# Two products for a column and its mirror image in the forward transforms along y

## The chip, the cores and the metric

The kernel runs on one core of a Trainium2 chip. A core has a matrix engine (TensorE, PE in the profile, with PEld for its weight loads), a vector engine (VectorE, DVE), a scalar engine (ScalarE, ACT), GpSimd (POOL), a queue engine that here issues the transfers (SyncE, SP), and 16 DMA engines. Matrix products land in PSUM, which here is eight banks of 512 fp32 values in each of 128 partitions; everything else is kept in SBUF or, between stages, in HBM. The engines run on their own and wait for each other on semaphores. The metric is the time of one execution on the device in microseconds (us).

## What is computed

The input is 4 images of 128 channels of 128 x 128 pixels. Layer 0 is a state-space layer over windows of 8 x 8 pixels. Layer 1 normalizes over channels and filters in the Fourier domain:

```python
z = (x - mu) / jnp.sqrt(var + 1e-05)
z = z * ln_gamma[None, :, None, None] + ln_beta[None, :, None, None]
Xf = jnp.fft.rfft2(z, axes=(-2, -1))
Phi = Phi_f_real + 1j * Phi_f_imag
Uf = Xf[:, :, None, :, :] * jnp.conj(Phi)[None, None]
U = jnp.fft.irfft2(Uf, s=(gx, gy), axes=(-2, -1))
S = jnp.einsum('bdlxy,lhd->bhxy', U, Theta)
H = jnp.einsum('bdxy,hd->bhxy', S, W1) + b1[None, :, None, None]
H = jax.nn.gelu(H, approximate=False)
out = jnp.einsum('bhxy,dh->bdxy', H, W2) + b2[None, :, None, None]
return x + out
```

What matters here is `rfft2`: for each image and channel a real 128 x 128 picture becomes 128 x 65 complex numbers. A Fourier transform along one axis is a product with a constant matrix of cosines and sines.

## The kernel before

There are four stages, one after the other. `mamba_layer` computes layer 0 and the normalized z, and leaves z in HBM as `zb`. `spectra` makes the forward transforms and leaves them in HBM as `xf`. `mix` multiplies by Theta and Phi for each of the 65 frequencies in y, leaving `sf`. `images_and_mlp` transforms back and applies the two last products. Each stage reads what the one ahead of it has stored. Instructions of an engine run in the order of the program text (`manual_schedule`); the waits between engines are put in by the framework, which tracks tiles. A pool's `bufs` is how many buffers a name rotates through: the next user of a buffer waits for the last reader of its previous content.

`spectra` is the only stage with edited instructions. For each of the four images b it has two parts.

Along x: `load` (line 491, on SP) brings blocks of 16 channels, 128 x 16 x 128 values, 1 MB, from `zb` into one of three z buffers. `along_x` (lines 497 and 498) takes four channels at a time: four matmuls of 128 x 128 into one PSUM bank `p1`, in four rotating banks, and one copy of 128 x 512 into the tile `a`, by ScalarE and VectorE in turn (`copies`, an endless cycle of the two). Channels lie closest in `a`, so the copy writes with a step of 512 bytes. Since z is real, the transform along x is kept as real parts of columns 0 to 64 and imaginary parts of columns 1 to 63: 128 columns of `a`. There are 32 such groups per image. `a` has a single buffer.

Along y: `along_y` (lines 500 to 513) takes three of the 128 output columns k at a time (KG = 512 // 130). For column k it uses m = min(k, 128 - k), the column's number or that of its mirror image, and makes two matmuls that accumulate in PSUM: the real column of `a` against `fy[:, KY : 3 * KY]`, and the imaginary column against one part or another of `fy`, whose sign depends on whether k is m or its mirror image. Columns 0 and 64 have no imaginary part and need one matmul. So an image has 2 + 2 x 126 = 254 matmuls along y, each with 130 result columns: 65 real parts and 65 imaginary parts. The two halves of a group are copied from PSUM to the tile x (line 511), the real parts by ScalarE and the imaginary parts by VectorE, again with a step of 512 bytes at the destination.

The tile x holds 64 columns, so an image has two of them (q = 0 and 1), each stored to `xf` by one DMA of 4160 KB (line 527). SP issues in program order: the loads of an image's first part, then its two stores, each of which waits for its tile x, and then the loads of the next image. Two blocks of the next image are asked for ahead of time, a third as the next image begins.

Of the other stages it is enough that `mix` starts with loads from `xf` (line 555), and that `idft_x`, `Phi_r` and `Phi_i`, constants prepared on the host, are indexed by the column along x.

Of the kernel before, what the change touches and what calls it, by code (L numbers as in the profile page):

```python
# [13 lines left out]
F32 = mybir.dt.float32  # L14
BF16 = mybir.dt.bfloat16
AF = mybir.ActivationFunctionType
ALU = mybir.AluOpType
PSUM = bass.MemoryType.PSUM

P = 128  # L20
# [6 lines left out]
W = 128  # L27
HB = 512
NL = 16
KY = W // 2 + 1  # L30
NG = WS * W // P


def mamba_layer(tc, d, x, x1, zb, deltas, dus):
# [429 lines left out]
def spectra(tc, d, zb, xf):  # L464

    nc = tc.nc  # L470
    B = len(zb)
    DG = 16
    CG, KG = HB // W, HB // (2 * KY)
    WH = W // 2
    with ExitStack() as ctx:
        ctx.enter_context(tc.manual_schedule())
        cp = ctx.enter_context(tc.tile_pool(name="f_const", bufs=1))
        sb = ctx.enter_context(tc.tile_pool(name="f_sb", bufs=2))
        ps = ctx.enter_context(tc.tile_pool(name="f_ps", bufs=4, space=PSUM))
        fx = cp.tile([P, W], F32, tag="fx", name="fx")  # L480
        nc.sync.dma_start(fx, d["dft_x"])
        fy = cp.tile([P, 4 * KY], F32, tag="fy", name="fy")
        nc.sync.dma_start(fy, d["dft_y"])
        loaded = {}
        copies = itertools.cycle((nc.scalar.copy, nc.vector.tensor_copy))

        def load(b, i):
            b, i = b + i // P, i % P
            if b < B:
                loaded[b, i] = sb.tile([P, DG, W], F32, tag="z", name="z", bufs=3)  # L490
                nc.sync.dma_start(loaded[b, i], zb[b][i : i + DG].rearrange("c x y -> x c y"))

        def along_x(b, i, a):
            z = loaded[b, i - i % DG]
            p1 = ps.tile([P, CG, W], F32, tag="p1", name="p_fx")
            for k in range(CG):
                nc.tensor.matmul(p1[:, k], z[:, i % DG + k], fx, start=True, stop=True)
            next(copies)(a[:, :, i : i + CG].rearrange("p k c -> p c k"), p1)

        def along_y(a, x, cols):  # L500
            p2 = ps.tile([P, KG, 2 * KY], F32, tag="p2", name="p_fy")
            for o, k in zip(range(KG), cols):
                m = min(k, W - k)
                single = m % WH == 0
                nc.tensor.matmul(p2[:, o], a[:, m], fy[:, KY : 3 * KY], start=True, stop=single)
                if not single:
                    by = fy[:, : 2 * KY] if m == k else fy[:, 2 * KY :]
                    nc.tensor.matmul(p2[:, o], a[:, WH + m], by, start=False, stop=True)
            n, at = len(cols), cols[0] % WH
            for r in range(2):  # L510
                next(copies)(
                    x[:, :, r, at : at + n].rearrange("p y k -> p k y"), p2[:, :n, r * KY : (r + 1) * KY]
                )

        load(0, 0)
        load(0, DG)
        for b in range(B):
            a = sb.tile([P, W, P], F32, tag="a", name="a", bufs=1)
            for i in range(0, P, CG):
                if i % DG == 0:  # L520
                    load(b, i + 2 * DG)
                along_x(b, i, a)
            for q in range(2):
                x = sb.tile([P, KY, 2, WH], F32, tag="x", name="x")
                for k in range(q * WH, (q + 1) * WH, KG):
                    along_y(a, x, range(k, min(k + KG, (q + 1) * WH)))
                nc.sync.dma_start(xf[:, :, b, q].rearrange("y c r x -> c y r x"), x)


def mix(tc, d, xf, sf):  # L530
# [179 lines left out]
@with_exitstack  # L710
def conv_kernel(ctx: ExitStack, tc: tile.TileContext, d, out):
    x = d["x"]
    B = x.shape[0]

    def images(name):
        return [tc.dram_tile([P, W, W], F32, name=f"{name}_{b}") for b in range(B)]

    x1, zb = images("x1"), images("z")
    xf = tc.dram_tile([KY, P, B, 2, 2, W // 2], F32, name="xf")
    sf = [tc.dram_tile([W, 2, KY, 2, P // 2], F32, name=f"sf_{b}") for b in range(B)]  # L720
    deltas, dus = (
        [[tc.dram_tile([P, WS * W], F32, name=f"{name}_{i}_{ch}") for ch in range(2)] for i in range(2)]
        for name in ("delta", "du")
    )
    mamba_layer(tc, d, x, x1, zb, deltas, dus)
    spectra(tc, d, zb, xf)
    mix(tc, d, xf, sf)
    images_and_mlp(tc, d, sf, x1, out)


def dft():

    w = np.exp(2j * np.pi * (np.outer(np.arange(W), np.arange(W)) % W) / W)
    h = w[:, :KY]

    s = w[:KY] * np.where(np.arange(KY) % (W // 2) == 0, 1, 2)[:, None] / W**2
    parts = {
        "dft_x": (h.real, -h.imag[:, 1:-1]),
        "dft_y": (h.imag, h.real, -h.imag, -h.real),
        "idft_x": (w.real, w.imag),  # L740
    }
    d = {k: np.concatenate(v, 1).astype(np.float32) for k, v in parts.items()}
    rows = np.r_[1 : KY - 1, 0, KY - 1]
    d["idft_y"] = np.concatenate((s.real[rows], -s.imag[rows[:-2]])).astype(np.float32)
    return d


def selectors():

    e = np.tile(np.eye(8), (1, NS))  # L750
    rsel, ssel = np.zeros((4, 4, 8, 4, P)), np.zeros((P, 4, 4, 8))
    for i in range(4):
        rsel[:, i, :, i] = e
        ssel[:, i, i] = e.T
    d = {"rsel": rsel.reshape(P, 4, P), "ssel": ssel.reshape(P, 4, 32), "center": np.eye(P) - 1 / P}
    return {k: v.astype(np.float32) for k, v in d.items()}


def layout(i):

    def col(a):
        return a.reshape(-1, P).T if a.ndim == 1 else a.reshape(-1, P, a.shape[1]).transpose(1, 0, 2)

    d = {"x": i["x"]}
    for k in "ln_g ln_b b_in conv_w conv_b W_x dt_b A_log D W_out b_out".split():
        d[k] = col(i[f"L0_conv_{k}"])
    d["W_in"], d["dt_w"] = i["L0_conv_W_in"], i["L0_conv_dt_w"]
    d["W_in_t"] = col(d["W_in"][:, : 2 * P].T).reshape(P, 2 * P)

    w = d.pop("W_x")  # L770
    d["W_xdt"] = w[..., :DR].transpose(2, 1, 0).reshape(DR, 2 * P)
    d["W_bc"] = np.repeat(w[..., DR:].reshape(P, 2, 2, NS), 8, -1)

    d["A_log"] = i["L0_conv_A_log"].reshape(32, 8, NS).transpose(2, 1, 0).reshape(P, 32)
    d["gamma"], d["beta"] = col(i["L1_conv_ln_gamma"]), col(i["L1_conv_ln_beta"])
    d["Theta"] = i["L1_conv_Theta"].transpose(2, 0, 1)
    d["Phi_r"], d["Phi_i"] = (i[f"L1_conv_Phi_f_{k}"].transpose(1, 0, 2) for k in ("real", "imag"))
    d["W1"], d["W2"] = i["L1_conv_W1"].T, col(i["L1_conv_W2"].T)
    d["b1"], d["b2"] = col(i["L1_conv_b1"]), col(i["L1_conv_b2"])
    return d | dft() | selectors()  # L780
# [18 lines left out]
```

## Time and profile before

| | us |
|---|---|
| median of three runs | 10449.41 |
| lowest and highest | 10445.54, 10451.61 |
| the profiled execution | 10450.79 |
| its span, first to last instruction | 10448.8 |
| window of the layer 0 stage, 0 to 7195 | 7195 |
| window of the forward transforms with the first loads of the next stage, 7195 to 7624 | 429 |
| window of `mix`, 7624 to 9632 | 2008 |
| window of `images_and_mlp`, 9632 to 10449 | 817 |

The span is the time on the engines; the small rest of the profiled execution lies around it. In the window from 7195 to 7624 TensorE is busy for 352.24 us, VectorE for 151.54, ScalarE for 151.89 and GpSimd for 0.00, with DMA at 0.58 of its capacity.

In the profile's lines an instruction is named by the line of the program that issues it, its engine, what it writes and reads, and its count. An entry "idle before" gives how long the engine stood idle just ahead of those instructions, and after the arrow what it was that released it. A matmul in fp32 leaves two records, since the number of records along y is 2032 for four times 254 matmuls. The chain of waits follows the work that ended last backwards: at each step to whatever released it, or to the instruction ahead of it on its engine.

### The profile page before, as it was taken

The numbers are of one execution on the slowest core, as the hardware profiler recorded it, in microseconds if no ns is written. First come the engines' busy times: TensorE is split into PE (matmuls) and PEld (weight loads), VectorE is DVE, ScalarE is ACT, GpSimd is POOL, SyncE is SP. The second block draws the span as 40 slices with busy tenths as digits, with TensorE's granted clock in tenths as the row PEclk, the third lists the DMA queues.
The fourth block names the chain that finished last, engine by engine and source line by source line (L and its number), as shares of the span: only waits on it lengthen the run. The fifth ranks groups of instructions, "written<-read, shape, count | busy, mean of one in ns | idle before, by whom it ended". The sixth has DMA issues, their size and how long they took to land.

```text
span 10448.8 us, 143616 instructions
## 1 busy us (share of the span) xinstructions
PE 9293.9 (89%) x48900; PEld 5027.3 (48%) x48900; DVE 8980.1 (86%) x7234; ACT 6524.3 (62%) x12463; POOL 8231.4 (79%) x4188
## 2 busy tenths in 40 slices
PE   6888888888888888888888888887889999998999
PEld 2333333333333333333333333335889999998766
DVE  5999999999999999999999999995389999998433
ACT  5776777777777777777777677773344444444433
POOL 5899998998998998989989899893079999997000
PEclk8999989989999999999999999997999999999999
DMA  4777677777776776777767767775521111112332
GB/s 150 213 229 220 213 223 218 217 219 219 225 221 213 226 222 214 223 217 225 221 210 228 218 215 223 219 221 160 148 68 34 35 35 36 36 36 62 136 128 93
DMA packets 1168110, 1794.06 MB, mean 172 GB/s; under 512 B 368641, under 2 KB 436497, under 8 KB 1166225
## 3 DMA queue, kind: packets, MB, share of 16 engines
q1 hardware_dynamic: 1167376, 1784.88, 56.6%
q8 instruction: 387, 6.34, 0.3%
q14 instruction: 347, 2.83, 0.1%
HBM read 1481.44 MB, written 303.04 MB: 171 GB/s over the span
## 4 chain that ended last, share of the span: by engine, by line
PE 58%; ACT 20%; DVE 9%; DMA 7%; issue 4%; POOL 1%; SPq 1%; DVEq 0%; ACTq 0%; POOLq 0%
PE p_v L578 13%; DVE hs L410 6%; PE p_du L376 6%; PE p_conv L202 5%; DMA dr<-delta 5%; ACT part L589 5%; PE p_bc L217 5%; PE p_dt L227 4%; PE p_y L428 4%; DVE p_du L408 3%; PE p_out L274 2%; ACT dA L391 2%; PE ln_cen L150 2%; ACT p_du L391 2%; PE p_h L672 2%
## 5 line engine op out<-in xcount | busy, mean ns | idle before, releaser
L418 POOL TENSOR_TENSOR hs<-hs,bc 128x1024 f32<-128x1024 f32 x2048 | 4806.3, 2372 | 408.9 <-DVE hs L410 357.3
L410 DVE TENSOR_TENSOR_SCAN hs<-dA,p_du 128x1024 f32<-128x1024 f32 x1600 | 3659.0, 2287 | 208.2 <-DVE p_du L408 4.9
L591 POOL TENSOR_TENSOR acc<-acc,part 128x512 f32<-128x512 f32 x1430 | 1829.3, 1319 | 640.6 <-ACT part L589 640.6
L408 DVE TENSOR_TENSOR p_du<-p_du,bc 128x1024 f32<-128x1024 f32 x1600 | 1935.8, 1210 | 219.6 <-PE p_du L376 215.0
L391 ACT ACTIVATE dA<-dr,A 128x504 f32<-128x504 f32 x3200 | 2072.0, 704 | 33.1 <-DVE hs L410 23.7
L578 PE MATMUL p_v<-theta,xk 128*128 128x128 f32 x16640 | 1941.4, 277 | 87.9 <-ACT part L589 51.9
L578 PEld LDWEIGHTS p_v<-theta,xk 128*128 128x128 f32 x16640 | 1883.1, 192 | 146.2 <-ACT part L589 118.9
L595 DVE SCALAR_TENSOR_TENSOR acc<-p_v,phi,acc 128x512 f32<-128x512 f32 x2470 | 1672.4, 740 | 114.2 <-PE p_v L578 87.5
L376 PE MATMUL p_du<-du,c_rsel 32*128 32x512 f32 x6400 | 1364.3, 678 | 370.2 <-DVE hs L410 370.2
L589 ACT ACTIVATE part<-p_v,phi 128x512 f32<-128x512 f32 x1430 | 904.8, 686 | 803.9 <-PE p_v L578 800.3
L428 PE MATMUL p_y<-hs,c_ssel 128*32 128x512 f32 x8192 | 1225.7, 634 | 134.2 <-DVE yz L263 82.9
L410 DVE TENSOR_TENSOR_SCAN hs<-p_du,ur 128x1024 f32<-128x1024 f32 x448 | 1019.0, 2275 | 86.8 <-ACT p_du L391 60.5
L356 POOL TENSOR_TENSOR ur<-ur,bc 128x1024 f32<-128x1024 f32 x448 | 1063.1, 2373 | 10.7 <-DMA ur<-du 10.7
L202 PE MATMUL p_conv<-tn,W_conv 128*128 128x512 f32 x2048 | 1007.3, 616 | 3.2 <-ACT xc L207 1.6
L376 PEld LDWEIGHTS p_du<-du,c_rsel 32*128 32x128 f32 x6400 | 370.4, 192 | 1081.1 <-issue 780.6
L227 PE MATMUL p_dt<-xc,W_dt 128*128 128x512 f32 x1024 | 619.8, 736 | 48.0 <-ACT dl L238 42.3
L391 ACT ACTIVATE p_du<-dr,A 128x504 f32<-128x504 f32 x896 | 613.9, 685 | 29.1
L428 PEld LDWEIGHTS p_y<-hs,c_ssel 128*32 128x32 f32 x8192 | 184.3, 111 | 887.5 <-issue 571.2
L207 ACT ACTIVATE xc<-p_conv,b_conv 128x512 f32<-128x512 f32 x256 | 176.2, 688 | 639.3 <-PE p_conv L202 639.3
L245 POOL TENSOR_TENSOR dl<-dl,ab 128x1024 f32<-128x1024 f32 x128 | 302.6, 2364 | 338.5 <-ACT ab L242 338.5
L202 PEld LDWEIGHTS p_conv<-tn,W_conv 128*128 128x128 f32 x2048 | 346.8, 189 | 455.2 <-issue 247.9
L168 PE MATMUL ln_back<-ident,cs 128*128 128x128 f32 x2048 | 339.5, 316 | 222.3 <-ACT cs L162 216.6
(100 smaller groups left out, 10341.0 us busy)
## 6 DMA issues: line engine op xcount, KB each, us to landing
dr<-delta SPq DMA_DIRECT2D x4096, 256.0 KB, 5.2
ur<-du SPq DMA_DIRECT2D x896, 256.0 KB, 6.4
delta<-dl SPq DMA_DIRECT2D x128, 512.0 KB, 2.9
du<-du SPq DMA_DIRECT2D x128, 512.0 KB, 5.4
xf<-x SPq DMA_DIRECT2D x8, 4160.0 KB, 16.4
xk<-xf SPq DMA_DIRECT2D x130, 256.0 KB, 3.8
sf<-acc SPq DMA_DIRECT2D x520, 64.0 KB, 1.7
s<-sf SPq DMA_DIRECT2D x8, 4160.0 KB, 13.4
```

What stands on the lines that cost most here:

```text
L202: nc.tensor.matmul(windows(o.pc), W_conv[:, ch, k], moved, start=(k == 0), stop=(k == K - 1))
L356: nc.gpsimd.tensor_tensor(fetched[s], fetched[s], both(o.bc[0], h), ALU.mult)
L376: nc.tensor.matmul(u.bank[:, j % 2], c["rsel"][p, u.i], half(u.o.du[p, u.ch], u.h), start=True, stop=True)
L391: nc.scalar.activation(u.dA[:, q, :, 1:], u.delta[:, q].rearrange("p (w t) -> p w t", t=L)[:, :, 1:], AF.Exp, scale=A[:, g : g + 1],)
L408: nc.vector.tensor_tensor(u.bu, u.bu, both(u.o.bc[0], u.h), ALU.mult)
L410: nc.vector.tensor_tensor_scan(u.hs.rearrange("p q t -> p (q t)"), u.dA.rearrange("p q w t -> p (q w t)"), u.bu.rearrange("p q t -> p (q t)"),
L418: nc.gpsimd.tensor_tensor(u.hs, u.hs, both(u.o.bc[1], u.h), ALU.mult)
L428: nc.tensor.matmul(o.py[h, ch][32 * j : 32 * j + 32], c["ssel"][:, u.i], units[s + j // 2].hs[:, j % 2], start=(u.i == 0), stop=False, ski ...
L578: nc.tensor.matmul(t[:, b], o.xk[:, b, r], theta[:, k], start=True, stop=True)
L589: nc.scalar.activation(part, v[of], AF.Copy, scale=factor)
L591: nc.gpsimd.tensor_tensor(apart, apart, part, ALU.add)
L595: nc.vector.scalar_tensor_tensor(mine, v[of], factor, mine, ALU.mult, ALU.add)
```

## The change

Column k and its mirror image 128 - k come from the same two products: one is their sum, the other their difference. After the change the two products of a column m from 1 to 63 are made once, each into a bank of its own (`pr` and `pi`), ScalarE copies `pr` to SBUF, VectorE adds `real` and `pi` into the tile x for column m, ScalarE copies `pi` to SBUF, and GpSimd subtracts `imag` from `real` into x for the mirror image. Columns 0 and 64 are made by `lone`.

```diff
-        ps = ctx.enter_context(tc.tile_pool(name="f_ps", bufs=4, space=PSUM))
+        ps = ctx.enter_context(tc.tile_pool(name="f_ps", bufs=3, space=PSUM))
...
-                loaded[b, i] = sb.tile([P, DG, W], F32, tag="z", name="z", bufs=3)
+                loaded[b, i] = sb.tile([P, DG, W], F32, tag="z", name="z", bufs=6)
...
-            p1 = ps.tile([P, CG, W], F32, tag="p1", name="p_fx")
+            p1 = ps.tile([P, CG, W], F32, tag="p1", name="p_fx", bufs=2)
...
         def along_y(a, x, cols):
-            p2 = ps.tile([P, KG, 2 * KY], F32, tag="p2", name="p_fy")
-            for o, k in zip(range(KG), cols):
-                m = min(k, W - k)
-                single = m % WH == 0
-                nc.tensor.matmul(p2[:, o], a[:, m], fy[:, KY : 3 * KY], start=True, stop=single)
-                if not single:
-                    by = fy[:, : 2 * KY] if m == k else fy[:, 2 * KY :]
-                    nc.tensor.matmul(p2[:, o], a[:, WH + m], by, start=False, stop=True)
-            n, at = len(cols), cols[0] % WH
-            for r in range(2):
-                next(copies)(
-                    x[:, :, r, at : at + n].rearrange("p y k -> p k y"), p2[:, :n, r * KY : (r + 1) * KY]
-                )
-
-        load(0, 0)
-        load(0, DG)
+            pr = ps.tile([P, KG, 2 * KY], F32, tag="pr", name="p_fy_r")
+            pi = ps.tile([P, KG, 2 * KY], F32, tag="pi", name="p_fy_i")
+            for o, m in enumerate(cols):
+                nc.tensor.matmul(pr[:, o], a[:, m], fy[:, KY:], start=True, stop=True)
+                nc.tensor.matmul(pi[:, o], a[:, WH + m], fy[:, : 2 * KY], start=True, stop=True)
+
+            def parts(t):
+                return t[:, : len(cols)].rearrange("p k (r y) -> p k r y", r=2)
+
+            def to(q):
+                at = q * (WH // 2) + cols[0] % (WH // 2)
+                return x[:, :, :, at : at + len(cols)].rearrange("p y r k -> p k r y")
+
+
+            real = sb.tile([P, KG, 2 * KY], F32, tag="real", name="real", bufs=3)
+            imag = sb.tile([P, KG, 2 * KY], F32, tag="imag", name="imag", bufs=3)
+            nc.scalar.copy(real[:, : len(cols)], pr[:, : len(cols)])
+            nc.vector.tensor_tensor(to(0), parts(real), parts(pi), ALU.add)
+            nc.scalar.copy(imag[:, : len(cols)], pi[:, : len(cols)])
+            nc.gpsimd.tensor_tensor(to(1), parts(real), parts(imag), ALU.subtract)
+
+        def lone(a, x):
+
+            p2 = ps.tile([P, KG, 2 * KY], F32, tag="pr", name="p_fy_r")
+            for o, m in enumerate((0, WH)):
+                nc.tensor.matmul(p2[:, o], a[:, m], fy[:, KY:], start=True, stop=True)
+                at = o * (WH // 2)
+                to = x[:, :, :, at : at + 1].rearrange("p y r k -> p k r y")
+                nc.scalar.copy(to, p2[:, o : o + 1].rearrange("p k (r y) -> p k r y", r=2))
+
+        for i in range(5):
+            load(0, i * DG)
...
-                    load(b, i + 2 * DG)
+                    load(b, i + 5 * DG)
                 along_x(b, i, a)
-            for q in range(2):
+            for h in range(2):
                 x = sb.tile([P, KY, 2, WH], F32, tag="x", name="x")
-                for k in range(q * WH, (q + 1) * WH, KG):
-                    along_y(a, x, range(k, min(k + KG, (q + 1) * WH)))
-                nc.sync.dma_start(xf[:, :, b, q].rearrange("y c r x -> c y r x"), x)
+                if h == 0:
+                    lone(a, x)
+                ms = range(max(1, h * (WH // 2)), (h + 1) * (WH // 2))
+                for k in range(0, len(ms), KG):
+                    along_y(a, x, ms[k : k + KG])
+                nc.sync.dma_start(xf[:, :, b, h].rearrange("y c r x -> c y r x"), x)
```

With it come a column order and its use: the first tile x holds columns 0 to 31 and their mirror images (64 standing with 0), the second columns 32 to 63 and theirs. The constants that are indexed by the column, `idft_x`, `Phi_r` and `Phi_i`, are put in the same order on the host, and `fy` shrinks from 4 x 65 to 3 x 65 columns. PSUM's eight banks are then two for `p1` and three each for `pr` and `pi`; z has six buffers, and five blocks of the next image are asked for ahead of time, a sixth as that image begins.

```diff
+COLS = np.arange(W // 2).reshape(2, 1, W // 4)
+COLS = np.concatenate((COLS, np.where(COLS > 0, W - COLS, W // 2)), 1).reshape(W)
...
-        "dft_y": (h.imag, h.real, -h.imag, -h.real),
-        "idft_x": (w.real, w.imag),
+        "dft_y": (h.imag, h.real, -h.imag),
+        "idft_x": (w.real[COLS], w.imag[COLS]),
...
-    d["Phi_r"], d["Phi_i"] = (i[f"L1_conv_Phi_f_{k}"].transpose(1, 0, 2) for k in ("real", "imag"))
+    d["Phi_r"], d["Phi_i"] = (i[f"L1_conv_Phi_f_{k}"].transpose(1, 0, 2)[COLS] for k in ("real", "imag"))
```

More of the change, by code (lines that the diff above doesn't have):

```diff
@@ L478, in spectra @@
         sb = ctx.enter_context(tc.tile_pool(name="f_sb", bufs=2))
-        ps = ctx.enter_context(tc.tile_pool(name="f_ps", bufs=4, space=PSUM))
+        ps = ctx.enter_context(tc.tile_pool(name="f_ps", bufs=3, space=PSUM))
         fx = cp.tile([P, W], F32, tag="fx", name="fx")
         nc.sync.dma_start(fx, d["dft_x"])
-        fy = cp.tile([P, 4 * KY], F32, tag="fy", name="fy")
+        fy = cp.tile([P, 3 * KY], F32, tag="fy", name="fy")
         nc.sync.dma_start(fy, d["dft_y"])
```

## The prediction

> **What bounds the kernel now.** I read the chain of waits first, to find where the edited function lies in the span, then a table of windows cut at its borders, then the groups by shape inside it. The forward transforms begin with the first matmul at 7195.28 us and end with the last store's issue at 7597.63: 402.35 of 10448.8 us. Nothing else runs there (POOL 0.00).
>
> ```profile
> core 0: us, PE busy (x) PEld busy (x) DVE busy (x) ACT busy (x) POOL busy (x), PEclk, DMA share, GB/s
> 7195.00:7228.00 33.00, 30.89 (x256) 30.41 (x256) 16.54 (x16) 16.66 (x16) 0.00 (x0) 0.95 0.98 276
> 7228.00:7286.00 58.00, 57.73 (x517) 57.76 (x518) 21.23 (x45) 21.35 (x44) 0.00 (x0) 1.00 0.27 76
> 7286.00:7332.00 46.00, 30.61 (x253) 30.29 (x252) 16.62 (x16) 16.66 (x16) 0.00 (x0) 0.85 0.97 273
> 7332.00:7389.00 57.00, 57.00 (x513) 57.00 (x512) 20.67 (x43) 21.30 (x44) 0.00 (x0) 1.00 0.28 78
> ```
>
> These are image 0 (along x, along y) and image 1. Along y TensorE is full and DMA nearly idle; along x DMA is full (0.97) and TensorE waits. Each DMA-bound stretch is a load queued behind the previous image's 4 MB store; the end is a store that the next stage waits for:
>
> ```profile
> 7286.58 19.86 DMA z<-z
> ...
> 7597.63 16.11 DMA xf<-x
> ...
> 7624.04 6.04 PE p_v L578 x32
> ```
>
> Groups by shape, then stretches of the timeline, one along y and one along x:
>
> ```profile
> L505 PE MATMUL p_fy<-fy,a 128*128 128x130 f32 x1024 | 197.0, 275 | 4.8 <-DVE a L498 4.8
> L508 PE MATMUL p_fy<-fy,a 128*128 128x130 f32 x1008 | 194.9, 275 | 0.0
> ...
> L511 DVE COPY x<-p_fy 128x195 f32<-128x195 f32 x168 | 83.4, 496 | 147.1 <-ACT x L511 147.1
> L498 ACT COPY a<-p_fx 128x512 f32<-128x512 f32 x64 | 66.6, 1041 | 111.7 <-PE p_fx L497 111.7
> ...
> L511 DVE COPY x<-p_fy 128x65 f32<-128x65 f32 x8 | 2.1, 264 | 0.0
> ```
> ```profile
> 7262.05 0.49 ACT L511 COPY x<-p_fy 128x195 f32<-128x195 f32 x1 [0.84 <-PE p_fy L508]
> ...
> 7262.57 0.49 DVE L511 COPY x<-p_fy 128x195 f32<-128x195 f32 x1 [0.83 <-ACT x L511]
> ```
> ```profile
> 7211.65 3.59 PE L497 MATMUL p_fx<-fx,z 128*128 128x128 f32 x30 [0.24 <-ACT a L498]
> 7212.81 1.05 ACT L498 COPY a<-p_fx 128x512 f32<-128x512 f32 x1 [1.24 <-PE p_fx L497]
> ```
>
> There are two records to a matmul, 2032 along y, so 254 matmuls per image. A full window (57.00 us, 513 records) gives 0.222 us each. Most important is the VectorE half of a group: all 168 of its full copies waited for ScalarE, and started 0.03 us after it ended, though both read finished products in the same PSUM tile. The two engines take turns on one bank. That does not come from the destination: line 498 writes interleaved columns of one tile from different PSUM tiles, and there an ACT copy (7210.55 to 7211.58) and a DVE copy (from 7211.44) overlap. Prices of operations, by line:
>
> ```profile
> L222 ACT COPY bc<-p_bc x256: 560/587/592, 88.8 to 7036.8; 128x512 f32<-128x512 f32 x128
> L263 DVE TENSOR_TENSOR yz<-p_y,zs x256: 665/666/693, 150.3 to 7167.3; 128x512 f32<-128x512 f32 x128
> L418 POOL TENSOR_TENSOR hs<-hs,bc x2048: 2336/2370/2470, 118.7 to 7158.6; 128x1024 f32<-128x1024 f32 x187
> L591 POOL TENSOR_TENSOR acc<-acc,part x1430: 1253/1274/2287, 7631.5 to 9629.5; 128x512 f32<-128x512 f32 x179
> L560 DVE TENSOR_TENSOR acc<-acc,acc x65: 1225/2273/2295, 7667.8 to 9630.8; 128x1024 f32<-128x1024 f32 x65
> ```
>
> [...] line 560, two SBUF inputs beside GpSimd, takes 2273 ns and at best 1225. The new add has one PSUM input. [...] Here copies with a 512-byte destination step cost (1041-264)/(512-65) = 1.74 ns an element, while the dense 128x512 of line 263 takes 666 ns in all.
>
> **The change part by part.**
>
> *TensorE along y.* 126 paired plus 2 lone matmuls instead of 254: 128 x 0.222 = 28.4 us an image instead of 56.5. A full group is 6 matmuls, 1.34 us, and now yields six columns.
>
> *Emptying a group.* Four instructions of 390 elements. (a) ScalarE copies pr, dense: 587 less 122 elements at 0.8 ns (from a 128x128 of line 157, 0.28 us) = 0.49 us. (b) VectorE adds real and pi into x: fixed part as in the strided copy, 264-65 x 1.74 = 0.15, plus 390 x 1.74 = 0.83 us; bounds 0.55 (no stride penalty) and 1.0. (c) ScalarE copies pi: 0.49. (d) GpSimd subtracts. Alone each is below 1.34. But b and c read the same bank, so c waits for b, and the next group's a is queued behind c on ScalarE, with VectorE waiting for that a: one chain a, b, c, a. With three gaps of 0.03 it is 0.49+0.83+0.49+0.09 = 1.90 us a group, above TensorE's 1.34. The three banks of pr and pi don't break it, since it is a queue order.
>
> *Sum along y.* 31 columns are 10 full groups and one of 1; 32 are 10 and one of 2. Per image 20 x 1.90 = 38.0, plus 1.0 (130 elements) and 1.5 (260 elements): 40.5 us. Ahead of it the two lone columns share a bank, so the second matmul waits for the first's copy (0.22+0.27+0.38+0.05), then 0.22, the first group 1.34 and 0.27 to its copy: 2.8 us.
>
> *GpSimd.* From 1274 and 2370 ns the slope is 2.14 ns; dense, 390 elements are 1.01 us. [...] no run shows strided writes. [...] I take 1.15[...]. Either is hidden below 1.90 and counts only as a tail of some 1 us at the store.
>
> *Banks along x.* p1 goes from 4 banks to 2. A bank's cycle is 1.16 (first matmul to copy, 7211.65 to 7212.81) + 1.045 copy + 0.07 = 2.28 us; two banks give 1.14 a group instead of 0.89. 32 groups: 36.5 us instead of 28.6. This is a loss of 7.9 an image, where DMA used to set 46.
>
> *Loads.* Six buffers let five blocks of the next image land during y, when DMA is at 0.27. Block 5 is still issued behind the store, and lands about 20 us after it (19.86 above), 21.5 after the chain's end; TensorE needs it after 18 groups and a copy, 18 x 1.14 + 1.1 = 21.6. So the DMA wait goes, just: its next candidate is this block, at 0 to 1 us. Per image DMA moves 8 loads and 2 stores, 17 MB at about 285 GB/s = 59 us, below the 80 of compute. Five loads stay in the first image's queue but its block 0 lands first, as now.
>
> *Nothing.* The column order changes constants only; later stages have the same instructions. Their start hangs on the last store, 26.4 us to the first matmul as now (bounds 0 and -4, were theta's load to start earlier).
>
> *Sum.* Image 0: x ends at 7234.4 (copies start at 7197.48, cold clock 0.5, 31 x 1.14, last copy 1.05), + 2.8 + 40.5 = 7277.7. Each later image 36.5 + 2.8 + 40.5 = 79.8; three give 7517.1, plus the GpSimd tail 1.0 = 7518.1 for the last store instead of 7597.63: 79.5 us earlier. 10448.8 - 79.5 = 10369 as span. The profiled run took 10450.79; the median, 10449.41, is 1.4 below; so 10370.
>
> **Rivals.**
>
> A, the chain above: 10370; own range 10345 to 10400 (20 us from 0.2 us on b over 84 groups, the rest from x).
>
> B, ScalarE isn't held and TensorE sets y: 28.4 + 1.4 + 36.5 = 66.3 an image, last store about 7465: 10317. For it: every engine is below 1.34. Against: the 168 waits.
>
> C, writes to x are ordered as well, or GpSimd takes about 2.6: add, pi copy, subtract, next add in turn, 0.83+0.49+1.15+0.12 = 2.6 a group, 55 us along y, +59: 10429. Against: the overlap of the two copies of line 498.
>
> D, slower. GpSimd becomes the bound through its strided write. Its place is the subtract; to lose, y must take 40.5 + 79.5/4 = 60.4 us, or 60.4/21.3 = 2.8 us a subtract (21.3 full-sized groups), 4.6 ns an element over the dense price. At 3.5 us it gives 74.6 an image, +136: 10506. For it: no strided GpSimd write is in the trace. Against: the penalty seen on both other engines is 0.7 ns.
>
> **How the numbers follow.** A 0.62, B 0.16, C 0.14, D 0.08. Leaving out D and most of C, the range is 10312 to 10420. Faster by over 0.2% (20.9 us, about what a measurement of this kernel can tell from no change) means below 10428.5: all of A and B and, as C spreads from about 10400 to 10450, 0.10 of its 0.14: 0.88. Same: the other 0.04 of C and 0.01 of D's near end: 0.05. Slower: 0.07.
>
> **What would show it.** In the profile after: ScalarE's pi copy released by the VectorE add, a group every 1.9 us; the add near 0.83; GpSimd below 1.4 and waiting for ScalarE; TensorE along x waiting for line 498's copies about 0.25 a group; no 20 us wait for z after image 0. Wrong if groups come every 1.34 (B), if VectorE waits for GpSimd (C), or if the subtract is above 1.9 and sets the pace (D).

## The result, and the profile after

The changed kernel takes 10367.09 us (median of 4 runs, 10355.75 to 10370.1) where the kernel before takes 10447.69 (4 runs beside them): a ratio of 0.9923, 95% interval 0.9907 to 0.9938. The profiled execution took 10367.51 us with a span of 10365.7.

The forward transforms, measured from the first product along x to the last store's issue, took 402.35 us before. In the profile after, the window table cut at the borders of image 1 (along x, along y) and the groups by shape read as follows. In a window's line, after its bounds and length, stand the busy times of PE, PEld, DVE, ACT and POOL, then the granted clock, the DMA share and GB/s.

```profile
7277.60:7315.10 37.50, 32.93 (x240) 30.15 (x240) 16.65 (x17) 16.83 (x17) 1.15 (x2) 0.95 0.97 272
7315.10:7356.20 41.10, 36.17 (x272) 33.23 (x272) 17.52 (x22) 19.11 (x45) 20.57 (x21) 0.96 0.59 165
```
```profile
L524 POOL TENSOR_TENSOR x<-real,imag 128x390 f32<-128x390 f32 x80 | 82.0, 1025 | 266.4 <-ACT imag L523 139.1 <-issue 127.3
...
L522 DVE TENSOR_TENSOR x<-real,p_fy_i 128x390 f32<-128x390 f32 x80 | 66.9, 836 | 88.5 <-ACT real L521 88.5
...
L521 ACT COPY real<-p_fy_r 128x390 f32<-128x390 f32 x80 | 39.2, 490 | 7.6 <-PE p_fy_r L508 7.6
L523 ACT COPY imag<-p_fy_i 128x390 f32<-128x390 f32 x80 | 38.8, 485 | 72.2 <-DVE x L522 72.2
```

Image 1 along x now takes 37.5 us instead of 46, along y 41.1 instead of 57. TensorE makes 272 records in 41.1 us along y, where 513 filled 57.00 before, so it no longer sets the pace there. The two lines to compare are the last: ScalarE's copy of `real` waits for almost nothing but its products, its copy of `imag` waits 72.2 us, always for VectorE. The line of VectorE waits for ScalarE in turn. That is the chain, and the timeline shows its period (each bracket gives the idle time before the instruction and what ended it):

```profile
7245.21 0.48 ACT L523 COPY imag<-p_fy_i 128x390 f32<-128x390 f32 x1 [0.91 <-DVE x L522]
7245.59 0.49 ACT L521 COPY real<-p_fy_r 128x390 f32<-128x390 f32 x1
7245.77 1.03 POOL L524 TENSOR_TENSOR x<-real,imag 128x390 f32<-128x390 f32 x1 [0.76 <-ACT imag L523]
7246.11 0.85 DVE L522 TENSOR_TENSOR x<-real,p_fy_i 128x390 f32<-128x390 f32 x1 [0.94 <-ACT real L521]
7247.00 0.49 ACT L523 COPY imag<-p_fy_i 128x390 f32<-128x390 f32 x1 [0.92 <-DVE x L522]
```

From one copy of `imag` to the next it is 7247.00 - 7245.21 = 1.79 us (full groups come every 1.76 to 1.79), against 1.34 us of products.

The first product along x starts at 7197.24 and the last store is issued here:

```profile
7514.06 0.74 POOL L524 TENSOR_TENSOR x<-real,imag 128x260 f32<-128x260 f32 x1 [0.30 <-ACT imag L523]
7514.82 0.36 SPq L550 DMA_DIRECT2D xf<-x  x1
```

So the stage takes 317.6 us, 84.8 fewer. Layer 0, whose instructions are the same, happened to take 2.0 us longer in this execution, and what follows the last store took 2850.9 us as against 2851.2: 84.8 - 2.0 + 0.3 = 83.1, the difference of the two spans. Layer 0 varies by more than that: in the ten profiles of this study the stage's first product falls anywhere from 7175.6 to 7200.4. The stage repeats far better: image 0's part along x, with the same instructions, took 39.25 to 39.33 us in the five profiles of kernels that share it. Below, therefore, the stage is compared, and the times of whole executions stand beside it.

### The profile page after: what moved, and what is told of

Read it like the earlier page. It is cut to its first block, busy times and chain, and to the rows that moved or that the text cites. A ratio compares the mean times of both kernels' runs of the same rounds, so it can differ in the third digit from the quotient of the medians.

```text
span 10365.7 us, 141790 instructions
## 1 busy us (share of the span) xinstructions
PE 9227.1 (89%) x47892; PEld 4936.1 (48%) x47892; DVE 8965.4 (86%) x7146; ACT 6516.4 (63%) x12471; POOL 8317.4 (80%) x4276
## 4 chain that ended last, share of the span: by engine, by line
PE 60%; ACT 21%; DVE 8%; DMA 6%; issue 4%; SPq 1%; POOL 0%; DVEq 0%; ACTq 0%; POOLq 0%
PE p_v L601 13%; PE p_conv L206 7%; PE p_du L380 6%; DMA dr<-delta 5%; DVE hs L414 5%; ACT part L612 5%; PE p_y L432 5%; PE p_bc L221 5%; PE p_dt L231 5%; PE p_out L278 2%; DVE p_du L412 2%; PE ln_cen L154 2%; ACT p_du L395 2%; PE p_h L695 2%; PE p_o L704 2%
## 5 line engine op out<-in xcount | busy, mean ns | idle before, releaser
L422 POOL TENSOR_TENSOR hs<-hs,bc 128x1024 f32<-128x1024 f32 x2048 | 4804.7, 2370 | 410.4 <-DVE hs L414 357.9
L380 PE MATMUL p_du<-du,c_rsel 32*128 32x512 f32 x6400 | 1367.7, 679 | 368.0 <-DVE hs L414 368.0
```

Of the source, the lines that this page charges most:

```text
L380: nc.tensor.matmul(u.bank[:, j % 2], c["rsel"][p, u.i], half(u.o.du[p, u.ch], u.h), start=True, stop=True)
L422: nc.gpsimd.tensor_tensor(u.hs, u.hs, both(u.o.bc[1], u.h), ALU.mult)
```

## The experiments

All numbers of stages are from the first product along x to the last store's issue, from one profile each.

**ScalarE's copy of pi ahead of the add.** Theory: the two engines take turns on pi's bank, and the order of the two lines makes ScalarE wait. The edit:

```diff
-            nc.vector.tensor_tensor(to(0), parts(real), parts(pi), ALU.add)
             nc.scalar.copy(imag[:, : len(cols)], pi[:, : len(cols)])
+            nc.vector.tensor_tensor(to(0), parts(real), parts(pi), ALU.add)
```

> ScalarE's copy of pi is put ahead of VectorE's add. In the changed kernel a full group along y took 1.78 us and the stage, from the first product along x to the last store's issue, 317.6 us. Theory A (ScalarE is held behind the add, since both read pi's bank): ScalarE no longer waits for VectorE, groups come at TensorE's pace, 1.34 us; along y takes about 30 us instead of 41 an image, and the stage 270 to 278 us (the load behind the store may take back 2 us an image). Rival 1 (the pace is set by something else along y: GpSimd, the step of the writes into x, or x's writes being ordered): groups stay at 1.7 us or more and the stage stays within 5 us of 317.6.

Measured: stage 7175.6 to 7452.9, 277.3 us; the kernel 10312.14 us, ratio 0.9873 (0.9857 to 0.989) to the kernel before. The timeline along y, where line 522 is now the copy and line 523 the add:

```profile
7229.43 0.84 DVE L523 TENSOR_TENSOR x<-real,p_fy_i 128x390 f32<-128x390 f32 x1 [0.49 <-ACT imag L522]
7229.47 1.02 POOL L524 TENSOR_TENSOR x<-real,imag 128x390 f32<-128x390 f32 x1 [0.31 <-ACT imag L522]
7229.86 0.48 ACT L521 COPY real<-p_fy_r 128x390 f32<-128x390 f32 x1 [0.47 <-issue]
7230.24 0.49 ACT L522 COPY imag<-p_fy_i 128x390 f32<-128x390 f32 x1
7230.77 0.83 DVE L523 TENSOR_TENSOR x<-real,p_fy_i 128x390 f32<-128x390 f32 x1 [0.50 <-ACT imag L522]
7230.81 1.03 POOL L524 TENSOR_TENSOR x<-real,imag 128x390 f32<-128x390 f32 x1 [0.32 <-ACT imag L522]
```

Adds come 1.34 us apart, TensorE's pace; the operations last as long as before. The first bracket also settles what is shared: the add neither reads `imag` nor writes anything that the copy touches, and yet it is released by that copy. All that the two have in common is that both read `pi`. Reading the same tile is not enough: the add and the subtraction both read `real`, which lies in SBUF, and overlap (from 7229.43 and 7229.47). In the trace the turn is a wait of 0.49 to 0.50 us ahead of the add, released by the copy, and the waits between engines are put in by the framework; whether the chip itself would hold back one of two readers of a bank, no run here shows. The turns remain, but only VectorE now waits (77 times for that copy, 54.2 us in all), and its wait does not hold up TensorE.

**The banks.** Theory: with two banks for p1 TensorE waits for the copies along x. The edit, with the lone columns' tile also at two:

```diff
-            p1 = ps.tile([P, CG, W], F32, tag="p1", name="p_fx", bufs=2)
+            p1 = ps.tile([P, CG, W], F32, tag="p1", name="p_fx", bufs=3)
...
-            pr = ps.tile([P, KG, 2 * KY], F32, tag="pr", name="p_fy_r")
+            pr = ps.tile([P, KG, 2 * KY], F32, tag="pr", name="p_fy_r", bufs=2)
```

> PSUM banks dealt out otherwise: p1 three, pr two, pi three. Theory A: along x TensorE no longer waits for line 498's copies; image 0's part along x falls from 39.4 to about 31 us; in later images the loads behind the store take over (block 5 at about 21 us after the part begins), so 37.5 falls to about 34; groups along y stay at 1.78. Stage about 299 us. Rival (DMA or the copies set the part along x already): the stage stays within 5 us of 317.6. Second rival (two banks of pr are too few): groups along y above 1.8 us.

Measured: 7193.9 to 7498.2, 304.3 us (10350.89 in one run). Image 0's part along x ends at 7225.7, after 31.8 us, as expected. Later images gained less: from the first lone column of image 0 to that of image 3 it is (7455.74 - 7225.67)/3 = 76.7 us an image, where the changed kernel has (7472.34 - 7236.57)/3 = 78.6. That is 1.9 less, where 3.5 had been expected, so the stage missed the expected 299 by 5 us. A wait for loads takes most of the banks' gain back. In the waits of this kernel along the stage:

```profile
PE p_fx L501 <- DMA z<-z: 27.3, 4, 10.4
```

10.4 of it is the start; the other three waits take (27.3 - 10.4)/3 = 5.6 us each, which is what separates the 7.5 us gained in image 0 from the 1.9 of the others.

**The subtraction made twice.** Theory: GpSimd, at 1.03 us a group, is hidden. The edit repeats the line of the subtraction, so that line 525 does line 524's work again.

> GpSimd makes each subtraction twice. Theory A (GpSimd, 1.03 us a group, is hidden below 1.78): doubled, 2.06 and a gap of 0.03 exceed 1.78, so groups come every 2.1 us, the stage grows by 26 to 38 us. If GpSimd were already part of the chain that sets the pace, the stage would grow by the whole second pass, 1.03 us x 84 groups = 87 us. If it were far from it and buffered, by less than 10.

Measured: 7180.8 to 7527.2, 346.4 us, 28.8 more (10380.97 in one run). GpSimd's timeline:

```profile
7252.51 1.02 POOL L525 TENSOR_TENSOR x<-real,imag 128x390 f32<-128x390 f32 x1
...
7254.58 1.02 POOL L525 TENSOR_TENSOR x<-real,imag 128x390 f32<-128x390 f32 x1
...
7255.63 0.48 ACT L521 COPY real<-p_fy_r 128x390 f32<-128x390 f32 x1 [0.19 <-POOL x L525]
```

GpSimd runs without a gap, 2.07 us for two, and ScalarE now waits for it to free a `real` buffer (39 times, 11.5 us in all). The growth is a third of the added 87 us: the first 0.7 us a group fell into GpSimd's idle time. So once it exceeds the chain's period GpSimd sets the pace, as the slower-side rival had it, but at its real price it is far from that.

**The loads alone, and the loads undone.** How much of the 84.8 us comes from the six z buffers, and how much from the products? First the kernel before, with only the loads of the change:

```diff
-                loaded[b, i] = sb.tile([P, DG, W], F32, tag="z", name="z", bufs=3)
+                loaded[b, i] = sb.tile([P, DG, W], F32, tag="z", name="z", bufs=6)
...
-        load(0, 0)
-        load(0, DG)
+        for i in range(5):
+            load(0, i * DG)
...
-                    load(b, i + 2 * DG)
+                    load(b, i + 5 * DG)
```

> The kernel before with six z buffers and five blocks asked for ahead, and nothing else of the change. Theory A: the waits of some 20 us for z in images 1 to 3 shrink to about 4 each, along y stays at 56.7 an image; the stage falls from 402 to about 365 us, so that the loads alone make some 37 of the 85 us. Rival (the loads are needed only because the change shortens y; TensorE sets the pace of the old kernel): the stage stays within 10 us of 402.

Then the same lines the other way round in the changed kernel:

> The changed kernel with the old loads: three z buffers, two blocks asked for ahead. Theory A: in images 1 to 3 block 2 waits behind the store and lands some 21 us after the part along x begins, and six blocks at 4.56 us (two banks) follow: the part takes about 50 us instead of 37.5, groups along y stay at 1.78. Stage 350 to 360 us instead of 317.5. Rival (the shorter part along y leaves the store out of the way): stage within 10 us of 317.5.

Measured: 7200.43 to 7568.45, 368.0 us, for the loads alone (10421.92 in one run), and 7195.7 to 7555.6, 359.9 us, for the change without them (10406.98 in one run). The waits for z, of the first and the second:

```profile
PE p_fx L497 <- DMA z<-z: 22.7, 4, 10.8
```
```profile
PE p_fx L501 <- DMA z<-z: 50.9, 4, 14.3
```

After the first, the waits with the loads alone are (22.7 - 10.8)/3 = 4.0 us each, as expected. The loads alone bring 34.3 us, the rest of the change alone 42.5, both together 84.8. So each brings something without the other, and together they give 8.0 us more than the sum; where these 8.0 lie was not followed further.

**The add from SBUF.** With the copy of pi ahead, the add can read `imag` instead of `pi`. This asks whether VectorE and GpSimd get in each other's way when both read two SBUF operands. The profile before has a hint: line 560, two SBUF inputs on VectorE, took 2.27 us at 9608.96 beside line 591 of GpSimd, and 1.23 us at 9630.83, where it had waited until GpSimd ended.

```diff
-            nc.vector.tensor_tensor(to(0), parts(real), parts(pi), ALU.add)
             nc.scalar.copy(imag[:, : len(cols)], pi[:, : len(cols)])
+            nc.vector.tensor_tensor(to(0), parts(real), parts(imag), ALU.add)
```

> As with the copy of pi put ahead of the add (stage 277.3 us, groups at 1.34), but the add reads imag from SBUF instead of pi from PSUM, so that VectorE and GpSimd each read two SBUF operands at the same time. If they share a read path, the two take turns: add and subtract together 0.83 + 1.03 = 1.86 us a group, above TensorE's 1.34, the add's mean well above 0.84, and the stage near 320 us. If they don't: add at 0.84, groups at 1.34, stage within 5 us of 277.

Measured: 7178.2 to 7468.2, 290.0 us (10320.56 in one run). The groups by shape:

```profile
L524 POOL TENSOR_TENSOR x<-real,imag 128x390 f32<-128x390 f32 x80 | 118.0, 1514 | 200.7 <-ACT imag L522 200.7
L523 DVE TENSOR_TENSOR x<-real,imag 128x390 f32<-128x390 f32 x80 | 105.6, 1411 | 28.4 <-ACT imag L522 27.9
```

They do: the add goes from 836 to 1411 ns, the subtraction from 1025 to 1514. How they do it shows in the first group of image 0, where both find their inputs ready:

```profile
7221.68 0.84 DVE L523 TENSOR_TENSOR x<-real,imag 128x390 f32<-128x390 f32 x1 [4.31 <-ACT imag L522]
7221.78 1.50 POOL L524 TENSOR_TENSOR x<-real,imag 128x390 f32<-128x390 f32 x1 [77.80 <-ACT imag L522]
...
7239.18 11.75 POOL L524 TENSOR_TENSOR x<-real,imag 128x390 f32<-128x390 f32 x8
```

The add, 0.10 us ahead, takes its usual 0.84, and the whole delay falls on the subtraction. If each merely ran slower beside the other, this add would have been stretched too, so the lines speak for turns. Yet the subtraction ends 0.76 us after the add, sooner than its own 1.03, and eight subtractions in a row take 11.75 us, 1.47 a pair and not the 1.86 that I had expected of turns. That sum takes both instructions whole. In the changed kernel the add takes 382, 596 and 836 ns for 130, 260 and 390 elements, the subtraction 465, 741 and 1025: 1.75 and 2.15 ns an element beside a fixed part of 0.15 to 0.2 us. The parts that grow with the elements make 0.68 + 0.84 = 1.52 us, an estimate close to 1.47. Whether only these parts take turns, and on what, no run shows. With one operand in PSUM, in the run with the copy ahead, the same add took 0.84 us while the subtraction ran beside it at 1.02 (from 7229.43 and 7229.47 above); over all full groups of the run with both mends, below, the means are 847 and 1029 ns. So in these runs one operand from PSUM kept the two apart.

**Both mends together.** Copy of pi ahead of the add, and the banks as above:

> The copy of pi ahead of the add, and banks three for p1, two for pr, three for pi. With TensorE at its own pace in both parts (28.6 + 1.4 along x, 29.1 along y) an image needs about 59 us, as much as its DMA (8 loads and 2 stores, 59). Theory A: the block behind the store then sets the part along x, some 35 us; 64 to 65 an image, stage 254 to 264 us. Rival (three banks give nothing once the loads set the part along x): stage within 5 us of 277.

Measured: 7183.0 to 7449.1, 266.1 us; the kernel 10299.15 us, ratio 0.9872 (0.9857 to 0.9887). The chain of waits names the load behind the store three times:

```profile
7246.93 20.46 DMA z<-z
...
7313.66 20.41 DMA z<-z
...
7382.76 20.16 DMA z<-z
```

The load sets the part along x, as expected, and the banks still bring 11.2 us over the swap alone; the stage lies 2 us above the 254 to 264 that were expected.

**Seven blocks ahead.** In addition eight z buffers, with one block of an image still behind the store; `real` and `imag` with two buffers each.

```diff
-                loaded[b, i] = sb.tile([P, DG, W], F32, tag="z", name="z", bufs=6)
+                loaded[b, i] = sb.tile([P, DG, W], F32, tag="z", name="z", bufs=8)
...
-                    load(b, i + 5 * DG)
+                    load(b, i + 7 * DG)
```

> As the last, with eight z buffers and seven blocks asked for ahead (real and imag with two buffers each, for room). Only block 7 of an image is then behind the store, and lands some 22 us after the part along x begins, when it is needed at 25. Theory A: no wait for z after image 0, TensorE without pauses but for the handover, 59 to 61 us an image, stage 240 to 250 us. Rival (DMA's total is the bound and order doesn't matter): stage as in the last run, within 4 us.

Measured: 7183.44 to 7426.76, 243.3 us; the kernel 10280.03 us (4 runs, 10275.23 to 10283.82), ratio 0.9852 (0.9836 to 0.9868) to the kernel before, and the fastest of those tried. In its waits and in its windows along the stage:

```profile
PE p_fx L501 <- DMA z<-z: 10.6, 1, 10.6
```
```profile
7183.40:7215.00 31.60, 30.38 (x256) 30.23 (x257) 16.68 (x16) 16.65 (x16) 0.00 (x0) 0.95 1.05 291
7215.00:7244.00 29.00, 28.52 (x251) 28.20 (x252) 16.16 (x20) 18.04 (x43) 19.61 (x20) 1.00 1.03 286
7244.00:7427.00 183.00, 176.12 (x1544) 174.44 (x1542) 104.43 (x117) 108.98 (x190) 67.31 (x69) 0.99 0.87 243
```

The only wait for z is the very first. TensorE is busy for 235 of 243.6 us, so this stage has little left in this form, and DMA, whose share is 0.87 to 1.05, has little to spare.

## Why the prediction was right

*The chain a, b, c, a.* Right, and it is what set the pace along y: swapping two lines took 40.3 us off the stage. The prices were met: 0.490 and 0.485 for the copies (0.49 forecast), 0.836 for the add (0.83), both worked out from other shapes. The period was about 1.78, not 1.90, because two instructions of ScalarE in a row overlap: the next copy of `real` starts 0.38 us after a copy of `imag` that lasts 0.48 to 0.49, so 0.10 of it and a gap of 0.03 drop out. Over 20 full groups that is more than 2 us an image. The last image's part along y, with the tail, took 7514.82 - 7472.34 = 42.5 us, where the sum gave 44.3 (2.8 + 40.5 + 1.0). The second lone product did wait for the copy of the first, for 0.47 us in image 0, and started 7237.50 - 7236.57 = 0.93 us after the first product, 0.92 in the sum.

*GpSimd.* Right that it is hidden; the doubled subtraction shows the cover. The price was too high: 1.15 taken, 1.03 measured. What 1.15 put on top of the dense price was a guess of mine that no trace had shown; the dense 1.01, worked out from 1274 and 2370 ns in the profile before, was the right one.

*Banks along x.* Right: image 0 along x took 39.3 us to the first lone column, where the sum had 39.1; the granted clock of the first 3 us was 0.50 here too, and 0.98 after them. Later images took 37.5 as against 36.5. The handover was missing from the sum: after image 0 TensorE stood idle for 2.59 us, until VectorE's first copy into `a`, and its next 32 records took 5.47 us, more than the 3.6 of its full pace (an estimate from 120 records in 13.41 us in the run with both mends).

*Loads.* Right. No wait for z is left after the start:

```profile
PE p_fx L501 <- DMA z<-z: 10.3, 1, 10.3
```

Block 5, named as the next candidate, causes none here; when either part is shortened it appears, at some 1 us an image after the swap, at 5.6 us in the run with other banks and at the head of the chain with both mends.

*The sum.* The stage was to take 7518.1 - 7195.28 = 322.8 us and took 317.6. Two errors are opposite in sign: the chain's period (too long by some 2 us an image) and the handover to x (too short by 1). That the whole kernel, 10367 where 10370 was forecast, comes closer than its stage is luck: layer 0 happened to run 2.0 us longer, and it scatters by 25. (The 56.5 us of products an image before the change are 56.4 by the prediction's own figures, 254 x 0.222; nothing rests on it.)

*Rivals.* TensorE as the pace along y (B) would have brought a group every 1.34 us, and they came every 1.78; but it is what the kernel becomes after the swap. Order among writes to x (C) isn't there: VectorE never waited for GpSimd in the changed kernel, and the add at 7246.11 starts while the subtraction that began at 7245.77 still runs. The slow subtraction (D) is excluded by 1025 ns, where 2.8 us would have been needed. One figure in the case against D was misread: by estimate the step costs about 0.7 ns an element on VectorE (1.74 less the 1.0 that line 263 leaves, 666 ns less a fixed 150 over 512 elements), but on ScalarE it is 1.74 less the 0.8 of the dense copies, about 0.9.

## What to carry to other kernels

In this program two engines that read the same PSUM tile took turns in program order: all 168 full copies of VectorE waited for ScalarE's before the change, and all 88 copies of `imag` for the add after it. Where a kernel's trace shows such waits, count them in, and write the reader first whose engine has the next group's work queued behind it. Price a stage by the chain through its engines' queues and not by the busiest engine: here no engine needed more than 1.34 us a group, and the group took 1.78. When a part shrinks, recount the loads behind its stores: the buffers for loads were worth 34 us by themselves and 42 on top of the rest (359.9 against 317.6), and with two more, and with the two mends, nothing waited for a load but the first product.

## What was not expected of the hardware

GpSimd's two-input operation did not suffer from a step of 512 bytes in its output: 1025 ns for 390 elements, where the line through its dense operations of 512 and 1024 elements (1274 and 2370 ns, in the kernel before) gives 1013, and 2.15 ns an element over its three sizes, where that line has 2.14. With the same step the copies of ScalarE and VectorE take 1.7 ns an element (264 to 278 ns for 65 elements, 1040 for 512, in the kernel before). Why GpSimd's rate did not change with the step was not tested.

VectorE and GpSimd with two SBUF inputs each delayed each other by less than their full lengths: a pair took 1.47 us instead of 1.86, and in the first group the add, which started first, kept its own 0.84 us.
